# Inverses of chunk blocks in groups of six instead of eight, finished ahead of their use, and a look-ahead of the block work that grows from 16 to 24 units

## The chip, the core and the metric

The kernel runs on one core of a Trainium2 chip. The core has a matrix engine (TensorE, PE in the profile; its weight loads are PEld), a vector engine (VectorE, DVE), an activation engine (ScalarE, ACT), a general engine (GpSimd, POOL) and a queue engine (SyncE, SP) that here issues nearly all DMAs. [...] The metric is the device time of the whole program in microseconds. All arithmetic is float32.

## The reference

There are 4 sequences of 4096 tokens with 512 features, 16 heads of 32. Each token's head vector is normalised to unit length (`rk`); the write key `wk` is that of the token before. A delta rule runs over time, for every sequence and head with a 32 x 32 state `S`:

```python
def step(S, inp):
    rk_t, wk_t, v_t, g_t, b_t = inp
    pred = jnp.einsum('bhk,bhkd->bhd', wk_t, S)
    err = (v_t - pred) * b_t[..., None]
    S = S + wk_t[..., None] * err[..., None, :]
    o = jnp.einsum('bhk,bhkd->bhd', rk_t, S) * g_t[..., None]
    return (S, o)
...
x = x + _layernorm(_L0_attn_ref(_layernorm(x), Wv, Wo, Wg, Wb))
x = x + _layernorm(_L0_ffn_ref(_layernorm(x), weight, ln_gamma, ln_beta))
```

The second layer is a matrix product with weights rounded to -1, 0 and 1, on inputs that are scaled by the largest absolute value of all tokens and clipped.

## The kernel before, in words

The time axis is cut into 128 units of 32 tokens; one unit holds all four sequences, so a tile has 128 rows. Work on a unit falls into two halves.

The *block half* depends on no other unit. It loads and normalises x, turns it (`keys_turn`), computes the values (`values`, `values_rest`), the Gram products of the keys (`grams`), masks them (`blocks`, `masked`) and stores the results to device memory (`hT_d`, `v_d`, `nat_d`). From the masked block of a unit and head, a 32 x 32 unit triangular matrix, its inverse is made by substitution on DVE: `invert(g)` treats a group of units at once and issues 30 pairs of a product (`pr`, L364) and an add (`na`, L370), and one copy (L375), 61 instructions. The pair number s works on `np_ * s * (31 - s)` elements in each row, where `np_` is half the number of units of the group. `gather` brings a group's blocks into the tile `na` (two buffers), `keep` stores the inverses to `q_d`, and `fetch_inverse` reads them back two steps before they are used.

The *chain half* runs over the units in order, as the state S passes through it: `predict` (PE ps_r L439, then DVE r L445), `apply` with the inverse (PE ps_u L455), `errors` (PE ps_f L468, then DVE e L471 and o L476), and `grow` (PE ps_ds L491, then DVE state L497). Behind it come the output projection (`project`, PE ps_wo L534), the first residual, the second layer (`ternary_a`, `ternary_b`, PE ps_y L593) and the final sum (`finish`).

The order on every engine is written out by hand. The list `steps` holds pairs (i, k): i is the chain's unit, k the unit of the blocks. There are four kinds of step. A `lead` step (10 at the start) does blocks alone. A `plan` step does one unit of chain and one of blocks. A `beside` step does blocks alone while the chain is under way; it follows a plan step, and the two together are called a pair below. A `late` step does the chain alone, when no blocks are left. A beside step is put in as long as k is less than i + FAR. Each step is a list of functions, and numbers between them (0.38, 0.2, 0.36, 0.06 in `plan`; 0.3 and 0.3 in `beside`; 0.65 and 0.35 in `late`) say what share of a step's inverse work is issued on DVE at that place; in the plan step of a pair these are multiplied by 1.4. An instruction of `invert` counts for 190 plus its elements, and instructions are issued at a place until the share that is due is reached. In `plan` the first share (0.38) stands between `x_stats` and `errors`: on DVE, the inverse instructions of this place stand ahead of e, which PE's ps_ds waits for. The second (0.2) stands ahead of the state's four adds, the last two behind them.

For each group, `spans` says from which step to which its inverses are computed: from two steps after its last block (or the end of the group before) to the step in which its first `fetch_inverse` stands.

Of the kernel before, what the change touches and what calls it, by code (L numbers as in the profile page):

```python
# [8 lines left out]
F32 = mybir.dt.float32  # L9
# [4 lines left out]
P = 128  # L14
# [8 lines left out]
def kernel(  # L23
# [24 lines left out]
    H = wg.shape[0]  # L48
# [18 lines left out]
    def bank(name):  # L67
        return psum.tile([P, 512], F32, tag="bank", name=name)
# [22 lines left out]
    def bcast(ap, shape, axis):  # L91
        return ap.unsqueeze(axis).to_broadcast(shape)
# [22 lines left out]
    with ExitStack() as ph1:  # L115
# [24 lines left out]
        stat = ph1.enter_context(tc.tile_pool(name="stat", bufs=6))  # L140
        cx = [{} for _ in range(NU)]

        sizes = [4, 4, 6, 6]
        NP = 4
        sizes += [2 * NP] * ((NU - sum(sizes)) // (2 * NP))
        sizes += [NU - sum(sizes)] * (sum(sizes) < NU)
        firsts = [sum(sizes[:g]) for g in range(len(sizes))]
# [89 lines left out]
        def values(i):  # L237
            my = cx[i]
            if i == 0:
                ps = bank("ps_g0")  # L240
                for k in range(KC):
                    nc.tensor.matmul(
                        ps[:, :H], lhsT=my["hT"][:, k, :], rhs=wvbT[:, k, D + H :],
                        start=(k == 0), stop=(k == KC - 1),
                    )
                my["gate"] = once.tile([P, H], F32, name="g0")
                nc.scalar.activation(my["gate"], ps[:, :H], AF.Sigmoid)
            my["v"] = wk.tile([P, D], F32, tag="v", name=f"v_{i}")
            my["ps_v"] = ps = bank(f"ps_v1_{i}")
            for k in range(KC):  # L250
                nc.tensor.matmul(  # L251
                    ps[:, : half + 2 * H], lhsT=my["hN"][:, k, :], rhs=wvbT[:, k, half:],
                    start=(k == 0), stop=(k == KC - 1),
                )
            gb = stat.tile([P, 2, H], F32, tag="gb", name=f"gb_{i}")
            nc.scalar.activation(
                gb, ps[:, half : half + 2 * H].rearrange("p (a h) -> p a h", a=2), AF.Sigmoid
            )
            gr = stat.tile([P, H], F32, tag="gr", name=f"gr_{i}", bufs=22)
            nc.sync.dma_start(out=gr[1:, :], in_=gb[: P - 1, 1, :])  # L260
            my["beta"], my["gate_next"], my["gr"] = gb[:, 0, :], gb[:, 1, :], gr

# [21 lines left out]
        def masks(i):  # L284
            return nc.vector if i < START - 4 else nc.gpsimd

        def writes(i):
            my = cx[i]
            bet = stat.tile([P, H], F32, tag="bet", name=f"bet_{i}", bufs=22)
            nc.gpsimd.tensor_tensor(bet, my["beta"], my["rn"], ALU.mult)  # L290
            nc.gpsimd.tensor_tensor(bet, bet, my["rn"], ALU.mult)
            my["bet"] = bet
            mb = wk.tile([P, H, DH], F32, tag="mb", name=f"mb_{i}", bufs=1)
            masks(i).tensor_tensor(
                mb.rearrange("p (j q) t -> p j q t", j=HQ),
                bcast(bet.rearrange("p (q j) -> p j q", j=HQ), [P, HQ, NQ, DH], 3),
                mneg.unsqueeze(1).unsqueeze(1).to_broadcast([P, HQ, NQ, DH]), ALU.mult,
            )
            my["mb"] = mb
# [46 lines left out]
        def gather(g, a):  # L346
            if a == 0:
                nas[g] = wk.tile([P, NP, DH, DH], F32, tag="na", name=f"na_{g}", bufs=2)
            for b in range(B):
# [5 lines left out]
        def invert(g):  # L355
# [4 lines left out]
            def product(s, prs):  # L360
                m = DH - 1 - s
                pr = wk.tile([P, NP * (DH // 2) ** 2], F32, tag="pr", name=f"pr_{g}_{s}", bufs=1)
                prs[s] = pr[:, : np_ * m * s].rearrange("p (a n t) -> p a n t", a=np_, n=s)
# [262 lines left out]
        def bring(name, w):  # L626
            r = wk.tile([P, NP, DH, DH], F32, tag="na", name=f"raw_{name}", bufs=2)
            r = r.rearrange("p a t s -> p (a t s)")[:, : KC * D]
            raws[name] = r = r.rearrange("p (o i) -> p o i", o=KC)
            src = w.rearrange("(o p) i -> p o i", p=P)  # L630
            nc.sync.dma_start(out=r, in_=src)
# [55 lines left out]
        def ternary_centre():  # L687
# [14 lines left out]
        plan = (  # L702
            (AHEAD, 4, load), (BACK, 2, fetch), (BACK, 2, fetch_inverse), (BACK, 2, again),
            (BACK, 0, predict), (AHEAD, -1, blocks), (AHEAD, -1, writes), (BACK, -1, out_turn),
            (BACK, -3, x1_turn),
            (BACK, 0, apply), (BACK, -3, x1_scale), (AHEAD, -1, masked),
# [4 lines left out]
            (AHEAD, 2, keys_turn), (AHEAD, -1, gates_first), (AHEAD, -2, gates), (BACK, 1, rekey), (BACK, -4, finish),  # L711
            (BACK, -1, project), (BACK, -3, largest), 0.36, (BACK, -2, x1_norm),
            (BACK, -1, residual), (AHEAD, 0, values), (AHEAD, 0, values_out, half),
            (AHEAD, 0, writes), (AHEAD, 0, values_rest), 0.06, (AHEAD, 0, values_out, 0),
            (AHEAD, 0, grams),
        )
# [10 lines left out]
        lead = (  # L727
            (AHEAD, 4, load), (AHEAD, -1, blocks), (AHEAD, 3, x_stats), (AHEAD, 1, key_sums),
            (AHEAD, 0, values), (AHEAD, 2, keys), (AHEAD, -1, writes), (AHEAD, 1, key_norms),
            (AHEAD, 2, key_squares), (AHEAD, -1, masked), (AHEAD, 0, values_out, half), 0.35,  # L730
            (AHEAD, 0, values_rest), (AHEAD, 3, x_norm), (AHEAD, 0, values_out, 0), 0.35,
# [3 lines left out]
        beside = (  # L735
            (AHEAD, 4, load), (AHEAD, -1, blocks), (AHEAD, 3, x_stats), (AHEAD, 1, key_sums),
            (AHEAD, 0, values), (AHEAD, 2, keys), (AHEAD, -1, writes), (AHEAD, 1, key_norms),
            (AHEAD, 2, key_squares), (AHEAD, -1, masked), 0.3, (AHEAD, 0, values_out, half),
            (AHEAD, 0, values_rest), (AHEAD, 3, x_norm), 0.3, (AHEAD, 0, values_out, 0),
# [1 line left out]
        )  # L741


        FAR = 4 * NP + 4
        START = sizes[0] + 6
        steps = [(None, k) for k in range(START)]

        k = START - 1
        for i in range(-2, NU - 1):
            k += 1  # L750
            steps.append((i, k))
            if i >= 0 and k < i + FAR:
                k += 1
                steps.append((None, k))
        at_k = {k: n for n, (_, k) in enumerate(steps)}
# [3 lines left out]
        def place(g, a):  # L759

            return a if sizes[g] == 2 * NP else 0

        for g, (f, n) in enumerate(zip(firsts, sizes)):
            begin = max(at_k[f + n] + 2, spans[-1][1] if g else 0)
            end = at_i[f - 2]
            assert begin < end
            spans.append((begin, end))

            free = spans[g - 2][1] + place(g - 2, sizes[g - 2] // 2 - 1) if g > 1 else 0
            for a in range(n // 2):  # L770
                free = max(at_k[f + 2 * a + 2], free)
                assert free < begin
                moves.setdefault(free, []).append((gather, g, a))
                moves.setdefault(end - 1 + place(g, a), []).append((keep, g, a))
                free += 1
# [225 lines left out]
```

## Time and profile before

| | |
|---|---|
| median of 3 runs | 2315.33 us (2312.81 to 2315.37) |
| the profiled execution | 2311.62 us, span of its instructions 2309.9 us |
| PE busy | 2219.5 us (96%) |
| DVE busy | 2027.3 us (88%), 3069 instructions |
| ACT, POOL busy | 1554.6 us (67%), 1528.3 us (66%) |
| inverses: L364 and L370 on DVE | 461.2 and 459.2 us, 540 instructions each |
| mean granted TensorE clock | 0.986 |

Busy time is the time in which an engine executes an instruction; waits are shown beside the instruction that waited. Windows are given in microseconds from the first instruction. The profiled execution is 3.7 us below the median of the runs; sums below are made against the profiled one and then moved by that difference.

### The profile page before, as it was taken

To read this page: it belongs to the slowest core of one execution; us is meant where nothing else is said; L and a number is where in the kernel's file an instruction comes from. 1 tells how busy PE (TensorE), PEld (TensorE's weight loads), DVE (VectorE), ACT (ScalarE), POOL (GpSimd) and SP (SyncE) were. 2 spreads that over 40 slices of the span, in tenths; PEclk is the share of its full clock that TensorE was granted. 3 is DMA by queue.
4 is the path that set the end of the run, shared out by engine and by line. 5 is a ranking of instruction groups with operands and counts; after the bars stand their busy time and mean duration, and the time that the engine had idled before them with its cause. 6 is when DMAs were issued, how large, how long until landed. Compare 5 with 4: busy or idle time off the path is not lost.

```text
span 2309.9 us, 60163 instructions
## 1 busy us (share of the span) xinstructions
PE 2219.5 (96%) x22563; PEld 1450.3 (63%) x22563; DVE 2027.3 (88%) x3069; ACT 1554.6 (67%) x3613; POOL 1528.3 (66%) x2057
## 2 busy tenths in 40 slices
PE   6688999999999999999999999999999999999997
PEld 5565666666666666666666666666666666655553
DVE  6898988999898998989989898899899898899853
ACT  6556676776776767767767677676776767655554
POOL 5787886777776776767767677676776766532221
PEclk9889999999999999999999999999999999999999
DMA  5586686777868777787877778677886967666652
GB/s 171 134 215 190 190 215 205 190 196 206 198 198 205 206 193 211 194 201 216 188 210 201 201 197 204 212 189 208 203 207 196 207 206 191 182 174 179 179 162 81
DMA packets 757202, 445.29 MB, mean 193 GB/s; under 512 B 582928, under 2 KB 582928, under 8 KB 756912
## 3 DMA queue, kind: packets, MB, share of 16 engines
q1 hardware_dynamic: 756528, 440.92, 71.7%
q8 instruction: 179, 2.93, 0.6%
q14 instruction: 111, 0.91, 0.1%
q10 hardware_dynamic: 384, 0.52, 0.1%
HBM read 205.07 MB, written 235.14 MB: 191 GB/s over the span
## 4 chain that ended last, share of the span: by engine, by line
PE 82%; DVE 11%; POOL 2%; issue 2%; DMA 2%; ACT 1%; SPq 1%; ACTq 0%; DVEq 0%; POOLq 0%
PE ps_wo L534 18%; PE ps_y L593 16%; PE ps_v L251 10%; PE ps_v L279 8%; PE ps_ds L491 6%; PE ps_gram L319 5%; PE ps_r L439 5%; PE ps_u L455 4%; DVE pr L364 3%; PE ps_hT L196 3%; PE ps_oT L514 2%; DVE na L370 2%; PE ps_f L468 2%; PE ps_xn L514 2%; DVE st_a L110 1%
## 5 line engine op out<-in xcount | busy, mean ns | idle before, releaser
L593 PE MATMUL ps_y<-wq,xn 128*128 128x512 f32 x1024 | 494.6, 606 | 0.0
L330 ACT COPY nat<-ps_gram 32x512 f32<-32x512 f32 x512 | 295.3, 577 | 286.6 <-PE ps_gram L319 276.1
L364 DVE TENSOR_TENSOR pr<-na 128x336 f32<-128x336 f32 (+25 forms) x540 | 461.2, 854 | 11.3
L370 DVE TENSOR_TENSOR na<-na,pr 128x336 f32<-128x336 f32 (+25 forms) x540 | 459.2, 850 | 12.2
L534 PE MATMUL ps_wo<-woT,oT 128*128 128x512 f32 x1024 | 464.0, 596 | 0.7 <-ACT oT L527 0.7
L231 POOL TENSOR_TENSOR rn<-ss,mhalf 128x16 f32<-128x16 f32 x128 | 440.7, 3443 | 10.7
L497 DVE TENSOR_TENSOR state<-ps_ds,state 32x512 f32<-32x512 f32 x508 | 348.4, 686 | 19.7 <-PE ps_ds L491 13.5
L338 POOL TENSOR_TENSOR nat<-nat,mb 128x512 f32<-128x512 f32 x122 | 159.5, 1307 | 290.6 <-issue 223.7
L534 PEld LDWEIGHTS ps_wo<-woT,oT 128*128 128x128 f32 x1024 | 185.3, 191 | 188.2 <-issue 184.7
L251 PE MATMUL ps_v<-wvbT,hN 128*128 128x288 f32 x1024 | 279.2, 417 | 14.3 <-POOL hN L207 14.2
L593 PEld LDWEIGHTS ps_y<-wq,xn 128*128 128x128 f32 x1024 | 174.5, 190 | 149.3 <-issue 146.0
L251 PEld LDWEIGHTS ps_v<-wvbT,hN 128*128 128x128 f32 x1024 | 198.1, 195 | 110.8 <-issue 28.2
L279 PE MATMUL ps_v<-wvbT,hN 128*128 128x256 f32 x1024 | 243.4, 381 | 0.0
L99 POOL TENSOR_TENSOR rstd_b<-vpe_b,mhalf 128x1 f32<-128x1 f32 x128 | 104.9, 820 | 186.3 <-ACT vpe_b L105 186.3
L279 PEld LDWEIGHTS ps_v<-wvbT,hN 128*128 128x128 f32 x1024 | 195.8, 191 | 34.3 <-DVE xr L543 0.4
L445 DVE TENSOR_TENSOR r<-v,ps_r 128x512 f32<-128x512 f32 x128 | 87.8, 686 | 135.0 <-PE ps_r L439 134.9
L520 ACT ACTIVATE junk_b<-ps_wo 128x512 f32<-128x512 f32 x128 | 76.5, 598 | 191.9 <-PE ps_wo L534 191.9
L491 PEld LDWEIGHTS ps_ds<-e,h 32*128 32x128 f32 x4064 | 127.3, 189 | 115.3 <-DVE e L471 91.1
L575 ACT ACTIVATE xn<-ps_xn,lnb,lng 128x128 f32<-128x128 f32 x512 | 193.6, 466 | 0.0
L491 PE MATMUL ps_ds<-e,h 32*128 32x128 f32 x4064 | 151.8, 286 | 19.3 <-DVE e L471 19.2
L319 PEld LDWEIGHTS ps_gram<-hT 32*128 32x128 f32 x4096 | 126.6, 187 | 39.5 <-issue 16.0
L319 PE MATMUL ps_gram<-hT 32*128 32x128 f32 x4096 | 151.1, 284 | 0.0
(153 smaller groups left out, 3867.6 us busy)
## 6 DMA issues: line engine op xcount, KB each, us to landing
x<-in_L_attn_x_dram SPq DMA_DIRECT2D x256, 128.0 KB
hT_d<-hT SPq DMA_DIRECT2D x128, 256.0 KB
v_d<-v SPq DMA_DIRECT2D x128, 256.0 KB
nat_d<-nat SPq DMA_DIRECT2D x128, 256.0 KB
na<-nat_d SPq DMA_DIRECT2D x256, 128.0 KB
q_d<-na SPq DMA_DIRECT2D x64, 512.0 KB
v<-v_d SPq DMA_DIRECT2D x128, 256.0 KB
hT<-hT_d SPq DMA_DIRECT2D x128, 256.0 KB
```

Source lines behind the costliest of these rows:

```text
L231: nc.gpsimd.tensor_tensor(rn, ss, mhalf, ALU.pow)
L251: nc.tensor.matmul(ps[:, : half + 2 * H], lhsT=my["hN"][:, k, :], rhs=wvbT[:, k, half:], start=(k == 0), stop=(k == KC - 1),)
L279: nc.tensor.matmul(ps[:, :half], lhsT=my["hN"][:, k, :], rhs=wvbT[:, k, :half], start=(k == 0), stop=(k == KC - 1),)
L319: nc.tensor.matmul(ps[:, j, q * P : (q + 1) * P], lhsT=hT[rows, q, :], rhs=hT[rows, q, :], start=True, stop=True,)
L330: nc.scalar.copy(nat[s].rearrange("p (j q) t -> p j q t", j=HQ), ps[s].rearrange("p j (q t) -> p j q t", q=NQ)[:, :, :, s],)
L364: nc.vector.tensor_tensor(prs[s], bcast(na[:, :, s, s + 1 :], [P, np_, s, m], 2), bcast(na[:, :, :s, s], [P, np_, s, m], 3), ALU.mult,)
L370: nc.vector.tensor_tensor(na[:, :, :s, s + 1 :], na[:, :, :s, s + 1 :], prs.pop(s), ALU.add)
L491: nc.tensor.matmul(psd[:, b, q * P : (q + 1) * P], lhsT=h[s, q * P : (q + 1) * P], rhs=e[s, q * P : (q + 1) * P], start=True, stop=True,)
L497: nc.vector.tensor_tensor(S[s, :, :, s], psd[s].rearrange("p b (q d) -> p b q d", q=NQ)[:, :, :, s], S[s, :, :, s], ALU.add,)
L534: nc.tensor.matmul(ps, lhsT=oT[:, k, :], rhs=woT[:, k, :], start=(k == 0), stop=(k == KC - 1))
L575: nc.scalar.activation(xn[:, k * P : (k + 1) * P], ps[:, k * P : (k + 1) * P], AF.Identity, bias=lnb[:, k : k + 1], scale=lng[:, k : k + 1],)
L593: nc.tensor.matmul(my["ps_y"], lhsT=my["xn"][:, k * P : (k + 1) * P], rhs=wq[:, k, :], start=(k == 0), stop=(k == KC - 1),)
```

## The change

Half a full group (`NP`) becomes 3 instead of 4, so that from the third group on all groups have six units instead of eight: 22 groups instead of 18. The look-ahead `FAR` was 4 * NP + 4 = 20 for all steps; it becomes a function of the chain's unit that gives 16 up to unit 32 and then one more with every ninth unit, to 24. The end of a group's inverses, which was the step of their first use, is drawn in to the step in which the blocks of the next group are there, and at least half a group's units after the beginning. Two small tiles that live from the block half to the chain half get 28 buffers instead of 22.

```diff
         sizes = [4, 4, 6, 6]
-        NP = 4
+        NP = 3
         sizes += [2 * NP] * ((NU - sum(sizes)) // (2 * NP))
...
-            gr = stat.tile([P, H], F32, tag="gr", name=f"gr_{i}", bufs=22)
+            gr = stat.tile([P, H], F32, tag="gr", name=f"gr_{i}", bufs=28)
...
-            bet = stat.tile([P, H], F32, tag="bet", name=f"bet_{i}", bufs=22)
+            bet = stat.tile([P, H], F32, tag="bet", name=f"bet_{i}", bufs=28)
...
-        FAR = 4 * NP + 4
+
+        def far(i):
+            return 4 * NP + 4 + min(8, max(0, (i - 24) // 9))
+
...
-            if i >= 0 and k < i + FAR:
+            if i >= 0 and k < i + far(i):
                 k += 1
                 steps.append((None, k))
...
             begin = max(at_k[f + n] + 2, spans[-1][1] if g else 0)
             end = at_i[f - 2]
+            if g + 1 < len(sizes):
+                end = min(end, max(begin + n // 2, at_k[f + n + sizes[g + 1]] + 2))
             assert begin < end
             spans.append((begin, end))
```

Counted through by hand from these loops, the steps are:

| | before | after |
|---|---|---|
| lead, plan, beside, late steps | 10, 111, 8, 18 | 10, 107, 12, 22 |
| pairs stand at chain units | 0 to 7 | 0 to 3, then 33, 42, 51, 60, 69, 78, 87, 96 |
| steps for one full group's inverses | 8 (the first group of eight: 6) | 6 (the last group: 14) |
| end of a group's inverses before its first use | 0 steps | 0 up to the seventh group, then 1 growing to 8 steps; the last group 0 |

## Prediction

> **What bounds the kernel now.** I read the page first, then the waits, then windows cut at the PE starts of `predict` (L439), which mark the chain's units.
>
> ```profile
> PE 2219.5 (96%) x22563; PEld 1450.3 (63%) x22563; DVE 2027.3 (88%) x3069; ACT 1554.6 (67%) x3613; POOL 1528.3 (66%) x2057
> DVE r L445 <- PE ps_r L439: 134.9, 113, 1.7
> PEld ps_ds L491 <- DVE e L471: 91.1, 95, 4.8
> ```
>
> PE is the bound, DVE the runner-up, and they wait for each other at two places in each unit: DVE reaches r early (about 1.2 us a time), PE reaches ps_ds close to e. The windows show where PE isn't the bound (us; PE, PEld, DVE, ACT, POOL busy; clock):
>
> ```profile
> 246.10:268.50 22.40, 22.40 (x232) 15.57 (x229) 19.37 (x32) 15.86 (x37) 19.29 (x28) 1.00 0.69 186
> 222.50:316.70 94.20, 90.34 (x916) 62.18 (x912) 85.74 (x137) 68.25 (x157) 82.09 (x108) 1.00 0.74 200
> 386.10:492.40 106.30, 102.60 (x1063) 66.89 (x1059) 102.74 (x147) 72.40 (x168) 79.76 (x96) 1.00 0.77 197
> 1037.90:1174.20 136.30, 136.13 (x1412) 89.15 (x1408) 123.20 (x181) 96.19 (x224) 96.74 (x128) 1.00 0.78 202
> 2025.80:2105.70 79.90, 73.24 (x748) 41.42 (x745) 76.52 (x101) 44.02 (x106) 24.24 (x34) 0.98 0.65 162
> 2129.40:2153.10 23.70, 23.70 (x250) 13.46 (x249) 21.31 (x35) 13.92 (x34) 6.28 (x10) 1.00 0.73 201
> ```
>
> From the first row a pair with PE full is 22.4 us; from the fourth a plan step is 17.01 (8 in 136.3, one of them 0.24 longer); from the last a late step is 11.85. Moving steps between these kinds is free for PE: a pair and a late step (34.2) stand for two plan steps (34.0). What counts is what exceeds these. Row 2, pairs 4 to 7: 94.2 - 4 x 22.4 = 4.6. Row 3, the group of eight that has only six steps: 106.3 - 6 x 17.01 = 4.2, with DVE 97% busy. Row 5, units 108 to 113: 79.9 - 6 x 11.85 = 8.8, DVE 96%. So DVE near 97% is DVE-bound. In row 4 it stands at 123.2 / 136.3 = 90%.
>
> One plan step, unit 56, shows the meeting at e (start, us, engine):
>
> ```profile
> 1141.10 0.69 DVE L445 TENSOR_TENSOR r<-v,ps_r 128x512 f32<-128x512 f32 x1 [1.47 <-PE ps_r L439]
> ...
> 1143.12 1.56 DVE L364 TENSOR_TENSOR pr<-na 128x792 f32<-128x792 f32 x1
> 1144.71 0.98 DVE L370 TENSOR_TENSOR na<-na,pr 128x792 f32<-128x792 f32 x1
> 1145.73 0.93 DVE L364 TENSOR_TENSOR pr<-na 128x736 f32<-128x736 f32 x1
> 1146.57 0.68 DVE L471 TENSOR_TENSOR e<-ps_f,bet 128x512 f32<-128x512 f32 x1
> ...
> 1147.31 1.17 PE L491 MATMUL ps_ds<-e,h 32*128 32x128 f32 x32 [0.17 <-DVE e L471]
> ```
>
> Three inverse instructions stand ahead of e; ps_ds starts 6.21 us after r, 5.97 in the other seven units: the 0.24. The first one always starts about 2.0 us after r and is 0.58 longer than its twin (1.56 against 0.98), beside a POOL multiply.
>
> **The change part by part.** *Price of an inverse instruction.* Alone, 60 elements take 0.22 us and 720 take 0.91: 1.045 ns an element and 0.16 fixed, with 0.03 between two. A group has 61 instructions and 9952 elements for each pair of units: six units 61 x 0.19 + 29856 x 0.001045 = 42.8 us, eight 53.2 (busy 56.3 in row 4, so 0.4 a step for the POOL encounters). Per plan step that is 42.8 / 6 + 0.4 = 7.5 instead of 7.0, and DVE is at (123.2 - 56.3) / 8 + 7.5 = 15.9 of 17.01: PE still bounds. Four more groups issue 244 more instructions, 46 us of fixed price on DVE. [...]
>
> *Plan steps.* I issued a group's instructions against the shares by hand. Ahead of e the six steps of a group then have 2.75, 3.16, 2.75, 1.88, 2.61, 2.63 us. In unit 56 it was 2.99 and 0.24 too much, so 2.75 is free. Only the second step is over: 0.41. It occurs 13 times outside pairs: 5.3; with two steps at the limit I take 6 (4 to 11). Gone: the old 0.24 (11 times) and 0.12 (3 times), -3.0.
>
> *Pairs removed.* Pairs 4 to 7 and the step behind them: 4.6 + 18.4 - 17.0 = -6.0.
>
> *Pairs added*, at units 33, 42, 51, 60, 69, 78, 87, 96. A pair issues two steps' inverse work, 1.4 in its plan step: 13.8, 15.0 or 11.3 us in turn (the third crosses the end of a group), against 10.7 on average in pairs 4 to 7, where 45.6 / 4 = 11.4 was measured on the tile na. So 14.5, 15.7, 12.0. DVE's other work there is (85.74 - 45.63) / 4 = 10.0. Its idle time was (94.2 - 85.74) / 4 = 2.1 in those pairs, and 0.6 a step where it was the bound (row 3); I take 1.3, as it becomes the bound but still waits for POOL's rstd. Sums 25.8, 27.0, 23.3 against PE's 22.4: 3.4, 4.6, 0.9, in all 3 x 3.4 + 3 x 4.6 + 2 x 0.9 = 25.8. DVE late means r late: queued behind it are ps_u and all of PE, and the stores on SP that wait for DVE. Behind the two group crossings a plan step gets 9.9 us of inverses: 8.4 + 9.9 + 0.4 + 0.6 = 19.2, +2.2 each. Together 30 (with idle 0.6 and 2.1: 24 to 37).
>
> *Pairs 2 and 3* get 14.7 and 13.9 instead of 11.2 and 11.0, as group 2 has six steps, not eight; there DVE idled 2.3 a pair, of which I let 1.0 absorb: +4 (0 to 6.5).
>
> *The six-step group of eight* goes: -4.2.
>
> *Late steps.* Where blocks have ended but shares haven't (8.8 before), the last group now has 14 steps, 3.3 us each, beside 6.7 of other DVE work: 10.0 of 11.85, free. Its two transition steps stay, 7.3 for 6.7 and 6.8 for 7.1: about 4.4 of the 8.8. -4.4.
>
> *Costed at nothing.* Earlier `keep` and inverses that wait in `q_d`: no row shows PE or DVE waiting for `tbd` or `q_d`, so there is nothing to win. SP issues as many DMAs as before (256 gathers, 64 keeps, 512 fetches); keeps move ahead of other stores on its queue by up to 8 steps, one 0.4 us issue each, covered by SP's slack; without it a late load would show as DMA ahead of st_a. POOL, ACT and PE do the same instructions.
>
> Sum: 30 + 6 + 4 - 3.0 - 6.0 - 4.2 - 4.4 = +22.4. Profiled 2311.6 gives 2334, the median 2315.3 gives **2338**.
>
> [...] At unit 2 PE waited 4.56 us for e and its next products took 2.09 us instead of 1.17; at unit 6 it waited 1.73 and they took 1.17.
>
> ```profile
> 180.18 2.09 PE L491 MATMUL ps_ds<-e,h 32*128 32x128 f32 x32 [4.56 <-DVE e L471]
> 278.69 0.50 PE L491 MATMUL ps_ds<-e,h 32*128 32x128 f32 x8 [1.73 <-DVE e L471]
> ```
>
> [...] In the added pairs up to 4.0 us stand ahead of e, 1.25 over the limit, so PE waits some 1.3 there. [...]
>
> **The rivals.**
> *Pairs absorbed (faster).* In the added pairs the smaller instructions slip into DVE's idle 2.1 us, and PE stays full. Place: r behind the beside step. Then +6 + 4 - 17.6 = -7.6, median 2308. It decides if the pairs and crossings cost under 7.6 in all, below 1 us a pair; against it: pairs 4 to 7 already cost 1.2 each with 3 us less DVE work.
> *Every plan step touched.* DVE's spare time before r falls from 1.6 to 1.1 us; if POOL encounters shift so that e or r is late by 0.25 in each of some 90 plan steps, +22 more: 2360. For it: 0.41 is at the limit already; against: in units 12 to 17, with far more work, the cost was only 0.7 each.
> *The change doesn't do what it says:* inverses do end up to 8 steps early, but nothing waited for them. Gains and losses could cancel (same) if pairs cost 1 to 2 us.
>
> **How the numbers follow.** Main case 0.74 (about 2322 to 2352, from the bounds +10 to +38), plan steps touched or pairs cold 0.11, cancelling 0.06, absorbed 0.09. Within 0.2% is 4.6 us, about what a measurement of this kernel can tell from no change. Slower 0.85, same 0.06, faster 0.09. The range 2321 to 2355 takes in the main case and a part of the worse one, and leaves out the other two.
>
> **What would show it.** Right: L364 and L370 with 660 instructions each, DVE busy up by some 45 us, PE about as before; predicts 25 to 27 us apart at units 33, 42, 60, 69, 87, 96, with DVE over 95% there; ps_ds waiting about 0.4 in one step of six; units near 105 cheaper. Wrong: 22.4 us at the pairs (absorbed), or most plan steps above 17.1.

## The result and the profile after

The changed kernel takes 2349.0 us (median of six runs) against 2314.5 for the kernel before, 34.6 us more. By the ratio it is slower by a factor of 1.0156 (95% interval 1.0144 to 1.0167), about 36 us. One of its six runs, 2582.6 us with a mean granted clock of 0.845, is left out of the ratio. The profiled execution took 2347.8 us, 36.2 more than that of before. The forecast was +22.4 us.

The page after. The first lines give busy time, share and instructions by engine:

```profile
span 2346.1 us, 60463 instructions
PE 2229.5 (95%) x22563; PEld 1454.2 (62%) x22563; DVE 2070.6 (88%) x3313; ACT 1556.5 (66%) x3613; POOL 1509.5 (64%) x2057
...
L364 DVE TENSOR_TENSOR pr<-na 128x504 f32<-128x504 f32 (+20 forms) x660 | 493.3, 747 | 16.8 <-issue 0.3
L370 DVE TENSOR_TENSOR na<-na,pr 128x504 f32<-128x504 f32 (+20 forms) x660 | 475.9, 721 | 14.3
```

PE issues the same 22563 products. DVE has 244 instructions more, and its busy time is up by 43 us. The products and adds of the inverses, 461 + 459 us before, take 493 + 476. PE's own busy time is up by 10 us, part of which is a lower clock (below): between 300 and 2280 us the granted clock was halved for 17.1 us, in the kernel before for 3.4. So the span grew by 36 us while PE's work stayed what it was: the question is where PE waits.

Windows of the first five later pairs with the steps behind them, up to the next step of ordinary length, then an ordinary stretch and the change to late steps. The columns are the window, its length, busy time of PE, PEld, DVE, ACT and POOL, granted clock, DMA share and GB/s:

```profile
723.00:767.20 44.20, 39.67 (x409) 26.73 (x404) 40.26 (x67) 29.45 (x67) 33.50 (x43) 1.00 0.79 185
886.70:932.20 45.50, 41.39 (x409) 27.25 (x404) 41.43 (x60) 29.21 (x67) 34.83 (x44) 0.96 0.65 181
1051.70:1093.30 41.60, 39.63 (x412) 26.77 (x411) 39.18 (x70) 29.45 (x67) 31.13 (x43) 1.00 0.71 205
1214.20:1261.20 47.00, 42.46 (x409) 28.55 (x406) 40.51 (x67) 29.46 (x67) 33.35 (x43) 0.93 0.78 179
1380.70:1442.20 61.50, 56.88 (x585) 37.79 (x581) 57.71 (x84) 41.13 (x95) 47.22 (x60) 1.00 0.70 186
...
364.10:466.60 102.50, 102.16 (x1063) 66.88 (x1059) 95.15 (x151) 72.15 (x168) 71.29 (x96) 1.00 0.77 202
2018.30:2118.50 100.20, 96.84 (x998) 54.43 (x994) 83.49 (x129) 56.90 (x137) 26.61 (x42) 0.98 0.66 172
```

A pair and one plan step need 22.4 + 17.0 = 39.4 us of PE. The pair at unit 33 took 44.2, that at 60, with the same instructions, 47.0. The row from 364.10 is one ordinary group, six plan steps: 102.50 us, 0.4 over 6 x 17.01 = 102.1, with DVE at 93%. The last row is the change to late steps, 8 units.

The account of the 36.2 us, from the PE starts of `predict` in both traces:

| place | before, us over PE's own time | after | difference |
|---|---|---|---|
| later pairs (8) and the step or two behind each | none | 39.1 | +39.1 |
| plan steps behind the two group crossings | none | 2.9 | +2.9 |
| second step of each group of six (12 times 0.41) | none | 4.9 | +4.9 |
| pairs 0 to 3 and unit 5 | | | +4.5 |
| pairs 4 to 7 and the step behind them | 6.0 | none | -6.0 |
| the group of eight with six steps | 4.2 | none | -4.2 |
| single stalls of 0.24 and 0.12 | 3.0 | none | -3.0 |
| first late steps | 8.8 | 5.4 | -3.4 |
| sum | | | +34.8 |

The rest, 1.4 us, is spread over the start and over steps longer by 0.01 to 0.03.

What happens behind a pair is seen best at unit 34. DVE, then PE, in the changed kernel (start, us, engine; in brackets the wait before it and what ended it):

```profile
748.51 0.67 DVE L445 TENSOR_TENSOR r<-v,ps_r 128x512 f32<-128x512 f32 x1
749.10 0.68 DVE L222 TENSOR_REDUCE ss<-sq 128x16 f32<-128x512 f32 x1
752.44 0.69 DVE L110 BATCH_NORM_STATS2 st_a<-x 128x6 f32<-128x512 f32 x1 [2.66 <-DMA x<-in_L_attn_x_dram]
...
753.27 1.46 DVE L370 TENSOR_TENSOR na<-na,pr 128x504 f32<-128x504 f32 x1
754.76 0.63 DVE L364 TENSOR_TENSOR pr<-na 128x450 f32<-128x450 f32 x1
755.43 0.63 DVE L370 TENSOR_TENSOR na<-na,pr 128x450 f32<-128x450 f32 x1
756.09 0.57 DVE L364 TENSOR_TENSOR pr<-na 128x390 f32<-128x390 f32 x1
756.57 0.69 DVE L471 TENSOR_TENSOR e<-ps_f,bet 128x512 f32<-128x512 f32 x1
```

```profile
757.31 1.17 PE L491 MATMUL ps_ds<-e,h 32*128 32x128 f32 x32 [2.92 <-DVE e L471]
```

DVE has no wait before r: it is the overloaded engine there, r comes 0.9 us late. But then it stands still for 2.66 us, though it is behind, because the statistics of x stand ahead of the inverse work and of e, and x hasn't landed (the product for the add at 753.27 was done at 748.25). The queue SP shows why; the last line is its longest wait in the last part of the pair (sum, count, longest):

```profile
741.55 0.35 SPq L546 DMA_DIRECT2D x_d<-xr  x1
...
742.94 0.39 SPq L273 DMA_DIRECT2D v_d<-v  x1
743.39 3.11 SPq L351 DMA_DIRECT2D na<-nat_d  x4
746.54 3.37 SPq L167 DMA_DIRECT2D x<-in_L_attn_x_dram  x4
...
SPq L546 <- DVE v L267: 2.6, 1, 2.6
```

The load of x for this step is issued at 746.54, in the pair's beside step, behind a store that waits 2.6 us for DVE and behind four gathers. (L546 stores the residual xr, which DVE finishes as it starts v; the view names v.) From the first of its four issues to the statistics that wait for it pass 5.9 us. Pairs 0 to 7 of the kernel before stood at other numbers of k: x is loaded two units at a time, when k is even, and there the even k was the plan step of a pair, a whole step earlier. Late r, late x and the lower clock are taken apart below.

### The profile page after: what moved, and what is told of

It is laid out like the page before. It is cut to its first block, busy times and chain, and to the rows that moved or that the text cites. A ratio compares the mean times of both kernels' runs of the same rounds, so it can differ in the third digit from the quotient of the medians.

```text
span 2346.1 us, 60463 instructions
## 1 busy us (share of the span) xinstructions
PE 2229.5 (95%) x22563; PEld 1454.2 (62%) x22563; DVE 2070.6 (88%) x3313; ACT 1556.5 (66%) x3613; POOL 1509.5 (64%) x2057
## 4 chain that ended last, share of the span: by engine, by line
PE 70%; DVE 19%; issue 3%; POOL 3%; DMA 2%; ACT 1%; SPq 1%; DVEq 0%; ACTq 0%; POOLq 0%
PE ps_wo L534 16%; PE ps_y L593 14%; PE ps_v L251 8%; PE ps_v L279 7%; PE ps_ds L491 5%; DVE na L370 5%; DVE pr L364 5%; PE ps_r L439 5%; PE ps_gram L319 4%; PE ps_u L455 4%; PE ps_hT L196 2%; PE ps_oT L514 2%; DVE state L497 2%; PE ps_f L468 2%; PE ps_xn L514 2%
## 5 line engine op out<-in xcount | busy, mean ns | idle before, releaser
L364 DVE TENSOR_TENSOR pr<-na 128x504 f32<-128x504 f32 (+20 forms) x660 | 493.3, 747 | 16.8 <-issue 0.3
L370 DVE TENSOR_TENSOR na<-na,pr 128x504 f32<-128x504 f32 (+20 forms) x660 | 475.9, 721 | 14.3
L231 POOL TENSOR_TENSOR rn<-ss,mhalf 128x16 f32<-128x16 f32 x128 | 421.5, 3293 | 10.7
L497 DVE TENSOR_TENSOR state<-ps_ds,state 32x512 f32<-32x512 f32 x508 | 348.3, 686 | 26.3 <-PE ps_ds L491 20.7
L251 PE MATMUL ps_v<-wvbT,hN 128*128 128x288 f32 x1024 | 281.0, 419 | 15.9 <-POOL hN L207 15.8
L455 PE MATMUL ps_u<-tbd,r 128*32 128x128 f32 x4096 | 138.4, 276 | 17.1 <-DVE r L445 13.5
```

The source lines that it names most:

```text
L231: nc.gpsimd.tensor_tensor(rn, ss, mhalf, ALU.pow)
L251: nc.tensor.matmul(ps[:, : half + 2 * H], lhsT=my["hN"][:, k, :], rhs=wvbT[:, k, half:], start=(k == 0), stop=(k == KC - 1),)
L364: nc.vector.tensor_tensor(prs[s], bcast(na[:, :, s, s + 1 :], [P, np_, s, m], 2), bcast(na[:, :, :s, s], [P, np_, s, m], 3), ALU.mult,)
L370: nc.vector.tensor_tensor(na[:, :, :s, s + 1 :], na[:, :, :s, s + 1 :], prs.pop(s), ALU.add)
L455: nc.tensor.matmul(ps[quarters(j), qq * P : (qq + 1) * P], lhsT=r[:, hd * DH : (hd + 1) * DH], rhs=tbd[:, j * NQ + qq, :], start=True, sto ...
L497: nc.vector.tensor_tensor(S[s, :, :, s], psd[s].rearrange("p b (q d) -> p b q d", q=NQ)[:, :, :, s], S[s, :, :, s], ALU.add,)
```

## The experiments

All times are medians, ratios are to the kernel before on the same chip. What is said of single steps comes from the one profiled execution of each kernel. Inverse work "from r to r" is what DVE executes between r of the pair's unit and r of the next.

**Loads of x one step earlier.** The last line stands twice in the kernel and is changed in both places.

```diff
-                xt = wk.tile([P, 2, D], F32, tag="x", name=f"x_{i}", bufs=2)
+                xt = wk.tile([P, 2, D], F32, tag="x", name=f"x_{i}", bufs=3)
...
-            (AHEAD, 4, load), (BACK, 2, fetch), (BACK, 2, fetch_inverse), (BACK, 2, again),
+            (AHEAD, 5, load), (BACK, 2, fetch), (BACK, 2, fetch_inverse), (BACK, 2, again),
...
-            (AHEAD, 4, load), (AHEAD, -1, blocks), (AHEAD, 3, x_stats), (AHEAD, 1, key_sums),
+            (AHEAD, 5, load), (AHEAD, -1, blocks), (AHEAD, 3, x_stats), (AHEAD, 1, key_sums),
```

> The changed kernel with the loads of x one step earlier (five units ahead instead of four, three buffers instead of two); nothing else moves. In the changed kernel's trace the eight later pairs and the two group crossings cost about 42 us over PE's own time. Behind the pairs at 33, 60 and 87 DVE's x_stats waits 2.4 to 2.7 us for an x that was only asked for in the beside step, e comes 2.9 us late, and after two of these waits PE runs at a lower clock for a while (2.9 and 1.7 us more). Theory A, this late load is a cost of its own beside DVE's overload: 3 x 2.9 + 4.6 = 13 us go, about 2336 us, and the step behind these three pairs falls from 20.7, 23.6 and 22.4 to about 18. Rival B, DVE is so far behind that the wait is covered by its backlog and something else makes e late: at most 3 us go, 2346 us or more.

Measured: 2337.1 us, 1.0104 (1.0087 to 1.0120): 11.9 us less than the changed kernel by the medians, 10.5 by the profiled executions. Theory A's 13 is met nearly, B is out. At the pairs at 33, 60 and 87, where DVE had waited for x, 12.0 us go; those at 42, 69 and 96, where it hadn't, gain nothing and lose 2.1 (the mean granted clock of the whole execution is 0.984, that of the changed kernel 0.985). All eight still cost 29.2 us. The step behind the pairs at 33, 60 and 87 takes 17.8 us, and the windows of 33 and 60, 44.2 and 47.0 before, are now equal:

```profile
723.20:764.40 41.20, 39.60 (x412) 26.77 (x412) 38.75 (x64) 29.30 (x67) 33.38 (x41) 1.00 0.86 187
1211.80:1253.00 41.20, 39.60 (x412) 26.77 (x412) 38.75 (x64) 29.32 (x67) 33.38 (x41) 1.00 0.85 183
```

**Pairs one unit later**, so that the load falls into the plan step of the pair.

```diff
-            return 4 * NP + 4 + min(8, max(0, (i - 24) // 9))
+            return 4 * NP + 4 + min(8, max(0, (i - 25) // 9))
```

> The changed kernel with every later pair one unit later (34, 43, ... 97), so that the x pair is loaded in the plan step of a pair and not in its beside step, 17 us before its use; two buffers as before. The inverse work in these pairs becomes 14.1, 13.9 and 14.7 us in turn instead of 13.8, 15.0 and 11.3, and no pair crosses a group's end. Theory A (late load beside overload): no wait of x_stats for x behind a pair, every pair costs 4 to 5 us by DVE's overload alone, about 36 in all against 42, about 2343 us. Rival B (the overload alone): eight pairs with 0.9 us more work each on average, minus the crossings' 3 us: +4 us, about 2353 us.

Measured: 2351.2 us, 1.0163 (1.0146 to 1.0180): nearer to B than to A. No wait for x is left behind a pair, as A said, but the pairs cost as much as before: 15.1 us of inverses from r to r on average instead of 14.3 makes r and e late by other ways. In the two steps behind the pair at 43, for instance, PE waits 0.7 us for v, then 0.9 for the residual and 1.2 for r. So this run doesn't tell the load from the overload; it changed both.

**No inverses in the last eight pairs.** The inverse instructions due there are passed over, so this kernel leaves out a part of the computation.

```diff
-                f(*args)
+                if f is add and args[0] not in prs:
+                    pass
+                elif f is add or not inv["skip"]:
+                    f(*args)
...
+            inv["skip"] = n >= 40 and (double or between_chain)
```

> The changed kernel, but in the last eight pairs no inverse instruction is issued on DVE: those that fall due there (about 120 of 1320) are left out of the computation. Everything else stands where it stood. If DVE's overload is the whole cost (rival B), the pairs take 22.4 us and the steps behind them 17.0: all of the 42 us go but for the crossings, about 2308 us. By theory A DVE reaches x_stats early and waits for x at all eight pairs, so that e is late by about 3 us each time, with a lower clock after some: 24 to 36 us of the 42 stay, 2330 to 2343 us.

Measured: 2312.2 us, 0.9992 (0.9983 to 1.0001). Pairs take 22.4 us and the steps behind them 17.0, but for 17.5 behind two. The window of unit 33 and the step behind it has PE full:

```profile
724.70:764.10 39.40, 39.40 (x410) 26.71 (x407) 27.52 (x51) 29.32 (x67) 28.57 (x43) 1.00 0.91 202
```

That is B's number, although the first experiment refuted B. Both hold once the load is read as a link, not as a cause beside the other: with DVE less busy (27.5 of these 39.4 us) the store ahead of x waits 0.8 us instead of 2.6, x is asked for some 3 us before `predict` at units 34, 61 and 88 instead of within 0.3 us of it, and the wait at unit 34 is 0.99 us where there is room for it:

```profile
750.50 0.69 DVE L110 BATCH_NORM_STATS2 st_a<-x 128x6 f32<-128x512 f32 x1 [0.99 <-DMA x<-in_L_attn_x_dram]
```

So theory A as I had put it, two costs that add, falls. Without inverse work in the pairs nearly all of the 39 us go; about a third of them pass through SP's queue. That an overload of DVE is needed for that third isn't shown by this run, as it takes away all inverse work at once; the last but one experiment looks at it.

**Look-ahead held at 16**, no later pairs.

```diff
-            return 4 * NP + 4 + min(8, max(0, (i - 24) // 9))
+            return 4 * NP + 4 + 0
```

> The changed kernel with the look-ahead held at 16: no pairs after unit 3, groups of six and drawn-in ends as changed. Theory A and B (the later pairs are the cost): their 42 us go; instead seven late steps carry a full share of inverses (6.7 + 7.2 of DVE work in 11.85 us), about +11 us: about 2318 us. Rival C, the smaller groups or the drawn-in ends cost everywhere: 2335 us or more, with plan steps above 17.1 us between.

Measured: 2320.3 us, 1.0032 (1.0020 to 1.0045), as expected to 2 us. Between the start and the late steps every sixth plan step is 17.42 us and the others are 17.01 or 17.02, so rival C is out. Six late steps are DVE-bound, 84.3 us instead of 6 x 11.85 = 71.1:

```profile
2101.20:2185.50 84.30, 71.92 (x747) 40.55 (x748) 82.17 (x122) 41.93 (x103) 22.84 (x31) 1.00 0.54 151
```

**Less inverse work ahead of e.**

```diff
-            (AHEAD, 2, keys), (AHEAD, 2, key_squares), 0.38,
+            (AHEAD, 2, keys), (AHEAD, 2, key_squares), 0.33,
...
-            (BACK, -1, project), (BACK, -3, largest), 0.36, (BACK, -2, x1_norm),
+            (BACK, -1, project), (BACK, -3, largest), 0.41, (BACK, -2, x1_norm),
```

> The changed kernel with the share of inverse work ahead of e cut from 0.38 to 0.33 in plan steps, and the share behind the state's adds raised from 0.36 to 0.41. Theory (DVE work ahead of e is what the second step of each group stalls on): counted against the shares, no plan step then has more than 2.75 us ahead of e (2.34 in the second step instead of 3.16), so the 0.41 us stalls at some 13 units go, 5 us, and in the pairs e is no longer late by 0.9 to 1.2 us; as DVE's total in a pair is unchanged, r comes as late as before and the pair itself gains nothing: about 2343 us. Rival (the pairs' loss sits at e): another 8 us, 2335 us. Rival 2 (the work only moves to the other meeting, at r): no gain, 2348 us.

Measured: 2339.7 us, 1.0109 (1.0088 to 1.0130), 9.4 less than the changed kernel by the medians, with single runs from 2335.3 to 2343.7. The trace decides more sharply: the profiled span is 2340.7 us against 2346.1, 5.4 less, and the twelve stalls of 0.41, 4.9 together, are gone. The pairs gain nothing in sum. The pair at 33 loses less at e (22.75 us instead of 23.41), but the step behind it takes 23.25 instead of 20.74: PE waits 2.0 us for r there instead of 0.7. With their steps the pair at 33 is 1.9 us longer than in the changed kernel, those at 51 and 78 0.7 each, those at 42 and 60 0.9 and 1.0 shorter, the others within 0.3. So the theory's 5 us is met place by place, and the first rival, a gain of the pairs at e, is out. Why the median fell by more than the profiled run isn't settled.

**Without the drawn-in ends.**

```diff
-            if g + 1 < len(sizes):
-                end = min(end, max(begin + n // 2, at_k[f + n + sizes[g + 1]] + 2))
```

> The changed kernel without the drawn-in ends: a group's inverses run until their first use, so a group with a pair in it has seven steps instead of six, and the last groups reach into the late steps. Inverse work in a pair falls from 11.3 to 15.0 us to about 12.2, so the later pairs should cost 1.5 to 2.5 us each instead of 5: some 25 us less. In return about 15 late steps carry a full share of 7.1 us beside 6.7 of other DVE work, where one over-full late step of the kernel with the look-ahead of 16 measured 14.4 us against 11.85: +2.5 each, some +35 us. Theory (drawing in the ends moves inverse work out of the late steps into the pairs): about 2355 to 2360 us, with cheap pairs and dear late steps. Rival (the drawn-in ends are themselves the loss): about 2325 us.

Measured: 2358.7 us, 1.0197 (1.0180 to 1.0215), as expected. The pair at 33 with its step is 42.0 us instead of 44.2, and fourteen late steps are over-full, 196.9 us instead of 14 x 11.85 = 165.9, with DVE 97% busy:

```profile
2023.50:2220.40 196.90, 167.85 (x1738) 94.66 (x1740) 191.92 (x286) 98.31 (x241) 52.10 (x71) 1.00 0.64 161
```

So the drawn-in ends save: they take inverse work out of the late steps. What they ask for it is paid in the pairs.

**Groups of six alone.**

```diff
-            return 4 * NP + 4 + min(8, max(0, (i - 24) // 9))
+            return 20
...
-            if g + 1 < len(sizes):
-                end = min(end, max(begin + n // 2, at_k[f + n + sizes[g + 1]] + 2))
```

> Groups of six alone: the look-ahead constant at 20 as before the change, no drawn-in ends. Theory: the six-step group of eight goes (-4), the 0.24 stalls go (-3) and 17 stalls of 0.41 come (+7), and the twelve late steps up to the last group's use carry 7.1 us of inverses: about 2.5 each against the 8.8 of before, +20: about 2333 us. Rival (smaller groups cost little, the loss is all in the look-ahead): 2312 to 2318 us.

Measured: 2330.0 us, 1.0072 (1.0055 to 1.0089). Sixteen units take 17.42 or 17.43 us, 0.41 more than the others, and eleven late steps (units 109 to 119) cost 26.5 us over 11.85 each, where before it was 8.8; 3 us under the sum expected. The smaller groups cost 17 us by themselves, and the late steps' 18 us more account for it: the gains and the new stalls among the plan steps nearly cancel.

**Lighter pairs**, with the earlier loads and the share of 0.33.

```diff
-                    inverses(1.4 * item if double else item)
+                    inverses(item)
...
-                    inv.update(ops=invert(g), done=0.0, due=0.0, steps=end - begin)
+                    twos = sum(
+                        i_ is None and m >= START for m, (i_, _) in enumerate(steps[:end]) if m >= begin
+                    )
+                    inv.update(ops=invert(g), done=0.0, due=0.0, steps=end - begin - 0.4 * twos)
```

> The changed kernel with the earlier loads of x, the share of 0.33 ahead of e, and a lighter pair: its plan step issues 1.0 instead of 1.4 shares (the beside step its 0.6 as before), and a group with a pair in it is divided by 5.6 instead of 6 steps. A pair then has about 12.2 us of inverses instead of 13.4 on average. Theory (DVE's total in the pair decides): 10.0 + 12.2 + 0.7 + 0.6 = 23.5 against 22.4, about 1 us a pair at twelve pairs; later pairs about 12 us in all instead of 42, plan steps without the 0.41: 2349 - 30 - 5 - 3 = about 2311 us. Rival (a pair costs 4 to 5 us whatever its inverses, by waits for POOL and ACT): about 2332 us.

Measured: 2314.5 us, 1.0005 (0.9996 to 1.0014). The later pairs take 22.4 or 22.5 us with 12.4 to 12.8 us of inverses from r to r, and the steps behind them 1 to 2.2 us too much in all. The rival's fixed price of 4 to 5 us for a pair doesn't exist.

**The same with the loads of x where they were.** The last of these lines stands twice in the kernel and is changed in both places.

```diff
-                xt = wk.tile([P, 2, D], F32, tag="x", name=f"x_{i}", bufs=3)
+                xt = wk.tile([P, 2, D], F32, tag="x", name=f"x_{i}", bufs=2)
...
-            (AHEAD, 5, load), (BACK, 2, fetch), (BACK, 2, fetch_inverse), (BACK, 2, again),
+            (AHEAD, 4, load), (BACK, 2, fetch), (BACK, 2, fetch_inverse), (BACK, 2, again),
...
-            (AHEAD, 5, load), (AHEAD, -1, blocks), (AHEAD, 3, x_stats), (AHEAD, 1, key_sums),
+            (AHEAD, 4, load), (AHEAD, -1, blocks), (AHEAD, 3, x_stats), (AHEAD, 1, key_sums),
```

> Lighter pairs and the share of 0.33 with the loads of x where they were (four units ahead, two buffers). With the full inverse work in the pairs the earlier loads were worth 12 us. Relay theory (DVE's lag holds SP's stores, and the load of x queued behind them comes late only because of that): with light pairs SP isn't held and the earlier loads are worth nothing, about 2315 us. Rival (a load issued in a beside step is too late by itself): 8 to 12 us more, 2323 us or more.

Measured: 2324.4 us, 1.0041 (1.0028 to 1.0055), some 10 us above the run with earlier loads. The relay theory is too strong: with light pairs SP is still held up. In the pair at 33 the store of the residual ahead of x waits 1.8 us for DVE, between the 2.6 of the changed kernel and the 0.8 of the pairs without inverses:

```profile
SPq L546 <- DVE v L267: 1.8, 1, 1.8
```

So x is asked for 1.0 us before `predict`, and the statistics wait 2.14 us for it, again 5.9 us after its first issue. The issue in the timeline:

```profile
742.73 2.04 SPq L167 DMA_DIRECT2D x<-in_L_attn_x_dram  x4
```

Only in the pairs without inverses was x asked for early enough: the load takes about 6 us in all three kernels (5.9, 5.9 and 6.2 at unit 34), and what differs is its start. So a load in a beside step comes too late with anything near a normal load on DVE; this wait is a cost that needs both, but no overload. Nearly half of the 10 us is what the steps behind the pairs at 60 and 87 took over that behind the pair at 33: 21.8 and 23.0 us against 19.9.

**A longer span for the last but one group**, on top of lighter pairs and earlier loads.

```diff
+            if g + 2 == len(sizes):
+                end = min(at_i[f - 2], end + 3)
```

> The lighter pairs, share of 0.33 and earlier loads, and in addition the last but one group gets nine steps instead of six, so that the last plan step and the first late step carry about 4.8 us of inverses instead of 7.3 and 6.8. With six steps the first late step measured 18.45 us against 11.85, by DVE work that makes r late and by a lower clock behind that wait. Theory: it falls to 13 to 15 us, 4 us less: about 2310 us, a gain over the kernel before that a measurement can just tell. Rival (that step is long for another reason): no change, 2314 us.

Measured: 2310.9 us, 0.9988 (0.9981 to 0.9995): the first late step falls from 18.45 to 13.60 us. It is the only version with the whole computation that lies below the kernel before, by 0.12%, less than what the forecast called telling; the interval narrowly excludes no change.

## Why the prediction was right or wrong

The forecast was 12 us low, and some 10 of that are one cost that it put at nothing, the loads of x. That 2349 lies within 2321 to 2355 is in so far luck: the range had room for a cost that wasn't foreseen.

*The bound and the two meetings.* Right. In plan steps PE stays the bound with 17.01 us. Apart from the second step of each group and the steps behind pairs and group crossings none was touched, and the rival that had every plan step late (2360) is out.

*Price of an instruction.* Right: the products and adds take 969 us against 920, and the ordinary group above has the forecast's 15.9 us of DVE work per step (95.15 / 6).

*Plan steps*, forecast 6 at 13 places with 0.41 each: 12 places, 0.41 each, 4.9. The count of instructions ahead of e against the 2.75 us that unit 56 allowed held to 0.01 us, and moving the share removed exactly these stalls.

*Gains.* -6.0, -4.2 and -3.0 came as forecast. The late steps gave -3.4, not -4.4.

*Pairs 2 and 3*, forecast +4: +4.5, of which 1.6 is a late r at unit 5.

*Pairs added*: the term that was mis-sized. Forecast 25.8, and 4.4 behind the crossings; measured 39.1 and 2.9. The sum of DVE's work was not the fault: in the three kinds of pair DVE took 24.3, 27.0 and 23.4 us from r to r, where the forecast had 25.8, 27.0 and 23.3, and with x in time all eight cost 29.2 us. The place was not as forecast: DVE is busy for 95 to 97% of the pairs named, but `predict` stands 23.4 to 23.8 us apart there, not 25 to 27. PE passes into the next step, and the larger part of the loss, 1.1 to 6.6 us, arises there, where r and e come late. What was missing is the load of x. The prediction followed the keeps on SP's queue and wrote of a late load that it "would show as DMA ahead of st_a", but it costed the loads themselves at nothing, as if the later pairs were copies of pairs 4 to 7. They aren't: at even k the load stands in the pair's other half. That is worth the 11.9 us of the first experiment, and some 10 with lighter pairs.

*The clock.* The forecast had "PE waits some 1.3" in the added pairs and put no loss of clock into its sum; its "pairs cold", at 0.11 together with the touched plan steps, are pairs behind whose waits the clock falls. The wait was 2.9 at units 34, 61 and 88, and the clock did fall in the last two; of the 2.5 us waits at units 43, 70 and 97 it fell at the first. Unit 34 and unit 61 have the same instructions; the first ran at a granted clock of 1.00, the second at 0.86. PE's ps_ds at unit 61 in the timeline (at unit 34, shown above, it took 1.17 us):

```profile
1248.47 2.09 PE L491 MATMUL ps_ds<-e,h 32*128 32x128 f32 x32 [2.93 <-DVE e L471]
```

And the windows of the two steps, of which the granted clock is the third number from the right:

```profile
746.50:767.20 20.70, 17.11 (x180) 11.10 (x176) 17.46 (x33) 12.16 (x29) 17.14 (x26) 1.00 0.88 206
1237.60:1261.20 23.60, 19.99 (x181) 12.97 (x178) 17.81 (x33) 12.21 (x29) 17.03 (x26) 0.86 0.84 191
```

Against unit 34 that is 2.9 us at unit 61 and 1.7 at unit 88 (22.4 us at 0.92); unit 43 (at 0.92) lost 1.65 against unit 70 (at 1.00), of which 0.64 came back in the step behind. So 5 to 6 of the 39 us are a lower clock.

How a wait behind which the clock fell differs from an equal one behind which it didn't can be read from the same trace. Its records of a halved clock begin at 916.49 us (unit 43), 1247.58 (61), 1742.51 (88) and 2036.06 (first late step); the distances are 97, 145 and 86 times 3.413 us. All 28 clock records of this trace, and all 20 of that of the kernel before, begin at whole multiples of 3.413 us behind the first of their trace, to 0.001 us. Cut at these times, the windows around the waits at units 34 and 61 are:

```profile
752.65:756.06 3.41, 1.74 (x5) 0.43 (x3) 3.30 (x5) 2.66 (x8) 3.25 (x4) 1.00 1.04 274
756.06:759.48 3.42, 2.17 (x38) 1.81 (x39) 3.35 (x7) 1.03 (x4) 3.34 (x4) 1.00 1.29 218
1244.17:1247.58 3.41, 1.37 (x4) 0.30 (x2) 3.27 (x6) 2.66 (x9) 3.33 (x3) 1.00 1.00 199
1247.58:1251.00 3.42, 2.53 (x35) 2.31 (x36) 2.77 (x6) 0.29 (x1) 3.34 (x4) 0.50 1.05 219
```

At unit 34 one of these times falls into the wait, and PE is busy for 1.74 and 2.17 us of the two windows; at unit 61 more of the wait falls into one window, PE is busy for 1.37, and the next window runs at half clock. The windows ahead of the other three drops have 0.90, 1.04 and 1.12 us; those of the waits at units 70 and 97, where the clock stayed up, at least 1.84 and 1.56. So the four drops came behind waits of 2.3 to 2.9 us, and behind windows in which PE was busy for 0.9 to 1.4 us.

*The rival "absorbed"*, pairs that cost next to nothing, is what happens with 12.4 to 12.8 us of inverses from r to r and x loaded earlier: its mechanism is real, but six of the eight pairs had 13.8 or 16.4 us.

## What to carry to other kernels

When two halves of a schedule are put into one step, work out the sum of the second-busiest engine for that step alone: here 90% over the steady state became 23.4 to 27.0 us of DVE time beside 22.4 of PE in eight places, and the queues behind that engine turned an overload of 1 to 4.6 us into 2 to 7.6. And look which loads are issued in a step that is shorter than the others: a prefetch "one step ahead" is only as early as the step is long, and x, asked for within 0.3 us of the step that uses it while it takes 6 us, cost 10 to 12 us of the 35. A copy of an existing pattern at another phase isn't the same pattern.

## What the runs showed of the hardware that was not expected

The clock of PE fell after two of three waits of 2.9 us and one of three of 2.5 us behind the pairs, and stayed up after the others. At half clock 32 products of ps_ds took 2.09 us instead of 1.17. The loss from such a wait therefore differs between places of one program: the steps at units 34 and 61, with the same instructions, took 20.7 and 23.6 us, at granted clocks of 1.00 and 0.86.

The clock records in the traces of the kernel before and of the changed one begin at multiples of 3.413 us from one another. Windows cut at these times, between 300 and 2280 us, give this count: in the five full-clock windows that were followed by half clock PE was busy for 26 to 43%, in the 1149 that were followed by full clock for 46% or more. The ends of PE's products are modelled, so these shares are rough.
